# A graph layer's edge loop: destination products from a DRAM table, one silu for two layers, 72 and 72 columns

## The chip, the cores and the metric

The kernel runs on one core of one Trainium2 chip. The metric is the device time of one execution, in microseconds. The core's engines work at the same time, each from its own instruction queue: TensorE (PE) multiplies matrices into PSUM, VectorE (DVE) and ScalarE (ACT) work element by element, GpSimd (POOL) issues the indirect gathers, and SyncE (SP) issues most other DMAs. Each engine's queue is worked off in order.

## The reference

One message-passing layer over 12500 nodes with 64 features and 400000 edges with 16 features, edges sorted by destination:

```python
m_in = concatenate([x[src], x[dst], edge_attr], axis=-1)       # 64 + 64 + 16
h = silu(m_in @ W1 + b1)                                       # 64
messages = silu(h @ W2 + b2)                                   # 64
agg = segment_sum(messages, dst, num_segments=12500)
out = layernorm(x + silu(concatenate([x, agg], axis=-1) @ W3 + b3))
```

Everything is in float32. W1 has three blocks of rows: W1a for the source, W1b for the destination, W1c for the edge's features, so that `m_in @ W1` is a sum of three products.

## The kernel before

Edges are worked off in tiles of 128, eight tiles to an octet (1024 edges), 391 octets (NO; the last has five tiles). Two tiles share the 128 partitions of one product: 64 features of the one above 64 of the other. Function `windows` builds everything; `general`, a fallback for other data, is not entered in these runs.

Edges are sorted by destination, so that an octet's destinations lie in a window of S = 48 nodes from a base node. For the destination's share of the first layer, `window_load` (SP) brings the window's 48 columns of transposed x, twice side by side, into `xr`; `window_product` (PE, L397) multiplies them with W1b into 96 rows; and `window_copy` (DVE, L402) multiplies by a mask that leaves the left half of the columns for one tile of a pair and the right half for the other, and writes the result into the first 96 rows of a 128x128 tile `xw`. The other 32 rows of `xw` hold W1c twice. There are three such tiles. `compare_dst` (DVE, L424) makes the one-hot rows `oh` that pick each edge's destination from the window, and the edges' features are loaded below them, so that a single matmul over 128 rows (`first_layer`, L441) adds destination and feature shares. `load` brings the destinations `dr` and the features once for every three octets.

The source's share has three ways. From octet RAW = 12, x W1a lies as a table `pa` in DRAM, and `gather` (POOL, L373) fetches 128 rows of it by one indirect DMA for each tile; first_layer adds them through the identity (L454). Some pairs of tiles are not gathered: `rows` fetches theirs with 16 single-row DMAs an octet on SP (L324), and `columns` copies columns of the transposed x, which is resident in SBUF as `xs`, one edge at a time into a tile `cx`, with DVE (L297) and ACT (L299); a matmul with W1a (L451) then takes its place. A pair of tiles has 256 columns. `ACOLS` = (32, 28) and `VCOLS` = (32, 32) say how many columns ACT and DVE copy in the two parts of an octet, together RATE = 124. Where an octet stands in the list `pairs`, its first two gathers are left out. Each copy's address comes from a register; the registers are filled by loads from an index tile `cxi` (L290), `LOADS` = (16, 8): sixteen in the first load of a part, eight in the others. DVE makes the addresses from the indices once for each pair of tiles (`address`, L359). In the first twelve octets the rows of x itself are gathered and multiplied.

The rest of `first_layer` is a silu on ACT with bias b1 (L458) into `h`. `second_layer` multiplies by W2 (L467, L469) and has its own silu (L473) into `m`. `add_up` (PE, L482) sums the messages with one-hot tiles `eh` from `compare_nodes` (DVE, L430), and `add_window` (DVE, L487) adds the window into `agg`. Finished nodes are worked off between the octets by the node steps (L504 to L552): statistics with L530, L533 and L534, division with L547.

The order on PE, ACT, DVE and SP is the program's order, under `tc.manual_schedule`; POOL's gathers run three octets ahead (AHEAD) in five buffers `ga`. In octet o the loop issues, among others: window_load(o+3), window_product(o+1), add_window(o-4), compare_dst(o+1), DVE's first columns, first_layer(o) with ACT's first columns before its silu, window_copy(o+1), compare_nodes(o+1), DVE's second columns, add_up(o-2), second_layer(o-1) with ACT's second columns before its silu, the addresses for octet o+2, and SP's rows.

Of the kernel before, what the change touches and what calls it, by code (L numbers as in the profile page):

```python
# [9 lines left out]
F32 = mybir.dt.float32  # L10
# [18 lines left out]
RAW = 12  # L29
TABLES = 7  # L30
ACOLS = (32, 28)
VCOLS = (32, 32)
ROWS = 16
LOADS = (16, 8)
XBASE = (0, 64 << 18)
XADDR = 36864
# [7 lines left out]
@with_exitstack  # L44
def kernel(
    ctx: ExitStack,
    tc: tile.TileContext,
    x: bass.AP,
    xt: bass.AP,
    src_c: bass.AP,  # L50
    src_row: bass.AP,
    dst_c: bass.AP,
    dst_row: bass.AP,
    attr_t: bass.AP,
    dst_2: bass.AP,
    attr_2: bass.AP,
    base: bass.AP,
    w1: bass.AP,
    b1: bass.AP,
    w2: bass.AP,  # L60
    b2: bass.AP,
    w3: bass.AP,
    b3: bass.AP,
    out: bass.AP,
    edges: int,
):

    nc = tc.nc
    N, D = x.shape  # L80

    const = ctx.enter_context(tc.tile_pool(name="const", bufs=1))
    dram = ctx.enter_context(tc.tile_pool(name="dram", bufs=1, space=DRAM))
    pa = dram.tile([N, D], F32, name="pa")
    badi = const.tile([1, 1], I32, name="badi")
    ident = const.tile([P, P], F32, name="ident")
    make_identity(nc, ident)

    with ExitStack() as inner:
        windows(inner, tc, ident, badi, pa, x, xt, src_c, src_row, dst_c, dst_row, attr_t, dst_2, attr_2, base, w1, b1, w2, b2, w3, b3, out, edges)  # L90

    flag = nc.values_load(badi[0:1, 0:1], min_val=0, max_val=2 * P,
                          skip_runtime_bounds_check_because="a count of partitions")
    with tc.If(flag > 0):
        general(tc, ident, x, xt, src_c, dst_c, dst_row, attr_t, w1, b1, w2, b2, w3, b3, out, edges)


def windows(ctx, tc, ident, badi, pa, x, xt, src_c, src_row, dst_c, dst_row, attr_t, dst_2, attr_2, base, w1, b1, w2, b2, w3, b3, out, edges):
# [33 lines left out]
    b1s = const.tile([P, 1], F32, name="b1s")  # L132
# [3 lines left out]
    for s in range(2):  # L136
        h = slice(s * D, (s + 1) * D)
        nc.scalar.dma_start(w1d[h, h], w1[0:D, :])
        nc.scalar.dma_start(b1s[h, :], b1.rearrange("(k o) -> k o", o=1))
# [65 lines left out]
    nc.vector.memset(mask[:, :D], 0.0)  # L205
    nc.vector.memset(mask[:, D:], 1.0)
# [29 lines left out]
    for k in range(3):  # L236
        t = fast.tile([P, P], F32, name=f"xw{k}")
        nc.vector.memset(t, 0.0)
        for q in range(2):
            nc.sync.dma_start(t[E + q * A:E + (q + 1) * A, q * D:(q + 1) * D], w1[2 * D:2 * D + A, :])  # L240
        xw.append(t)
# [6 lines left out]
    with tc.tile_pool(name="gat", bufs=AHEAD + 2) as gat, tc.tile_pool(name="drp", bufs=2) as drp, \  # L248
# [4 lines left out]
            tc.tile_pool(name="ps2", bufs=2, space=PSUM) as ps2, \  # L253
# [17 lines left out]
        def columns(o, eng, part):  # L271
            if o < RAW:
                return
            lo = (o - RAW) * RATE
            if eng == ENG.Activation:
                lo, n = lo + sum(ACOLS[:part]), ACOLS[part]
            else:
                lo, n = lo + sum(ACOLS) + sum(VCOLS[:part]), VCOLS[part]
            hi, todo = lo + n, n
            while lo < hi:  # L280
                j, e0 = lo // (2 * P), lo % (2 * P)
                if j >= len(pairs):
                    return
                n = min(hi - lo, P - e0 % P, LOADS[lo > hi - todo])
                if pairs[j] not in cols:
                    cols[pairs[j]] = cx.tile([P, P], F32, name="cx")
                t = cols[pairs[j]].bitcast(U8)
                s = e0 // P
                h = slice(s * D, (s + 1) * D)
                _, regs = nc.values_load_multi_w_load_instructions(  # L290
                    indices[j][0:1, e0:e0 + n], engines=(eng,), min_val=XBASE[s] + XADDR,
                    max_val=XBASE[s] + XADDR + 4 * (N - 1), skip_runtime_bounds_check_because="src names a node")
                for e, r in zip(range(e0 % P, e0 % P + n), regs):
                    to, frm = t[h, 4 * e:4 * e + 4], xb[h, ds(r - (XBASE[s] + XADDR), 4)]
                    if eng == ENG.DVE:

                        nc.vector.tensor_reduce(to, frm[:, :, None], AX.X, OP.max)  # L297
                    else:
                        nc.scalar.copy(to, frm)  # L299
                lo += n  # L300
# [85 lines left out]

        def window_load(o):
            if o % 4 == 0:
                bases(ENG.SP, o)
            xr = win.tile([D, 2, S], F32, name="xr")  # L390
            frm = xt[:, ds(winreg.pop((ENG.SP, o)), S)]
            nc.sync.dma_start(xr, frm[:, None, :].to_broadcast([D, 2, S]))
            winrow[o] = xr

        def window_product(o):
            pw = mis.tile([P, P], F32, name="mm")
            nc.tensor.matmul(pw[:E, :], winrow[o].rearrange("k s w -> k (s w)"), w1bb.rearrange("k s m -> k (s m)"),  # L397
                             start=True, stop=True)
            winrow[o] = pw

        def window_copy(o):
            nc.vector.tensor_tensor(xw[o % 3][:E, :], winrow.pop(o)[:E, :], mask[:E, :], op=OP.mult)  # L402

        def load(c, o0=0, o1=CT // OT):
# [6 lines left out]
            for k in range(2):  # L411
                nc.sync.dma_start(dr[k * S:(k + 1) * S, e], dst_2[k:k + 1, d].to_broadcast([S, e.stop - e.start]))
            nc.sync.dma_start(oh[E:, e], attr_2[:, d])

        hots = {}
# [18 lines left out]
        def first_layer(o):  # L434
# [5 lines left out]
            p1 = ps1.tile([P, OT // 2, P], F32, name="p1")  # L440
            nc.tensor.matmul(p1[:, :k], xw[o % 3], oh, start=True, stop=False, skip_group_check=True)  # L441
            if o < RAW:
# [4 lines left out]
                xg = work.tile([P, OT // 2, P], F32, name="m")  # L447
# [8 lines left out]
            columns(o, ENG.Activation, 0)  # L456
            h = work.tile([P, OT // 2, P], F32, name="h")
            nc.scalar.activation(h[:, :k], p1[:, :k], AF.Silu, bias=b1s)  # L458
            made[o] = h, eh

        def second_layer(o):
# [3 lines left out]
            h, eh = made.pop(o)  # L465
            p2 = ps2.tile([P, OT, D], F32, name="p2")
# [4 lines left out]
            columns(o + 1, ENG.Activation, 1)  # L471
            m = work.tile([P, OT, D], F32, name="m")
            nc.scalar.activation(m[:, :n2], p2[:, :n2], AF.Silu)  # L473
            made[o] = m, eh

        def add_up(o):
            c, t0, n, first, last = octs[o]
            m, eh = made.pop(o)
# [114 lines left out]
        tables = list(range(0, N, 8 * P))  # L593
        cuts = [SCT] + [min(t + 46 * OT, TILES) for t in range(SCT, TILES, 46 * OT)]
# [3 lines left out]
        with tc.manual_schedule(engines={ENG.PE, ENG.Activation, ENG.DVE, ENG.SP}):  # L598
            compare_dst(0)
            compare_nodes(0)  # L600
            for o in range(NO + 1):
# [32 lines left out]
                if o + 1 < NO:  # L634
                    window_product(o + 1)
# [9 lines left out]
                if o == 0:  # L645
                    nc.vector.tensor_copy(b2r, b2p[:, None, :].to_broadcast([3, OT, D]))
                if o + 1 < NO:
                    window_copy(o + 1)
                    compare_nodes(o + 1)
# [10 lines left out]
                if o >= 1:  # L660
                    for c in tables[(o - 1) * per:o * per]:
                        table(c)
                if o >= 2:
                    add_up(o - 2)
                if o >= 1:
                    second_layer(o - 1)
# [298 lines left out]
```

## Time and profile before

| quantity | value |
|---|---|
| median of 10 runs | 3438.23 us (3437.63 to 3441.43) |
| the profiled execution | 3438.32 us, span 3436.1 us |
| granted TensorE clock, mean | 0.774 |
| PE busy | 2527.6 us, 74% |
| DVE busy | 2505.9 us, 73% |
| ACT busy | 2743.8 us, 80% |
| POOL busy | 2573.2 us, 75% |
| DMA | 229.98 MB, 67 GB/s in the mean |

The span runs from the first to the last instruction of the profiled execution. Busy time is time in which the engine itself works; what its queue does alone (register loads, semaphore waits, issuing DMAs) is not in it. In the group lines, a count is followed by the busy time in us and the mean duration in ns of one instruction; since instructions overlap, count times mean can exceed the busy time. After the second bar stands the engine's idle time just before such instructions and what ended most of it. "issue" is idle time that ended without any semaphore that the profile shows. In the waits, the three numbers are the total in us, how often, and the longest. In the timeline, the numbers are start and length in us, and a bracket gives the idle time before the piece.

### The profile page before, as it was taken

The numbers are of one execution on the slowest core, as the hardware profiler recorded it, in microseconds if no ns is written. First come the engines' busy times: TensorE is split into PE (matmuls) and PEld (weight loads), VectorE is DVE, ScalarE is ACT, GpSimd is POOL, SyncE is SP. The second block draws the span as 40 slices with busy tenths as digits, with TensorE's granted clock in tenths as the row PEclk, the third lists the DMA queues.
The fourth block names the chain that finished last, engine by engine and source line by source line (L and its number), as shares of the span: only waits on it lengthen the run. The fifth ranks groups of instructions, "written<-read, shape, count | busy, mean of one in ns | idle before, by whom it ended". The sixth has DMA issues, their size and how long they took to land. (4 is left out here: it accounts for less than half of the span.)

```text
span 3436.1 us, 107486 instructions
## 1 busy us (share of the span) xinstructions
PE 2527.6 (74%) x15131; PEld 1788.9 (52%) x15131; DVE 2505.9 (73%) x26395; ACT 2743.8 (80%) x23402; POOL 2573.2 (75%) x2724
## 2 busy tenths in 40 slices
PE   6877877767777777777677776767767777777676
PEld 4555555545555455555454554545545555555454
DVE  2487768777787777777777777777777777777775
ACT  2388878788888788887888878888888787887884
POOL 7777777777777777777777777777777777777774
PEclk8887777787877777777777778787788787777777
DMA  6533333223233322323323332332232333233232
GB/s 124 126 65 64 62 66 62 62 59 70 62 65 70 64 60 61 70 61 61 70 61 67 68 66 59 63 68 60 62 69 64 68 67 62 61 61 69 59 73 47
DMA packets 203943, 229.98 MB, mean 67 GB/s; under 512 B 133612, under 2 KB 141988, under 8 KB 202324
## 3 DMA queue, kind: packets, MB, share of 16 engines
q1 hardware_dynamic: 101528, 122.61, 16.0%
q0 software_dynamic: 86880, 89.14, 14.1%
q10 hardware_dynamic: 14812, 11.26, 1.4%
q14 instruction: 595, 4.87, 0.5%
q8 instruction: 128, 2.10, 0.3%
HBM read 216.36 MB, written 6.40 MB: 65 GB/s over the span
## 5 line engine op out<-in xcount | busy, mean ns | idle before, releaser
L373 POOL DMA_INDIRECT ga<-pa,sc x2619 | 2480.1, 947 | 798.6 <-issue 711.7
L299 ACT COPY cx<-xs 64x4 uint8 x22560 | 2236.2, 189 | 142.8 <-issue 112.0
L297 DVE TENSOR_REDUCE cx<-xs 64x4 uint8 x24032 | 1774.5, 150 | 552.0 <-issue 472.9
L441 PE MATMUL p<-oh,xw 128*128 128x512 f32 (+1 forms) x782 | 627.8, 896 | 315.9 <-DVE xw L402 313.1
L454 PEld LDWEIGHTS p<-ident,ga 128*128 128x128 f32 x2620 | 477.1, 252 | 368.5 <-issue 329.2
L454 PE MATMUL p<-ident,ga 128*128 128x128 f32 x2620 | 512.1, 341 | 192.9 <-DMA ga<-pa,sc 191.9
L469 PE MATMUL p<-w2d,h 128*128 128x128 f32 x3126 | 579.2, 342 | 0.0
L469 PEld LDWEIGHTS p<-w2d,h 128*128 128x128 f32 x3126 | 487.7, 238 | 110.5 <-issue 110.5
L482 PE MATMUL pg<-eh,m 128*64 128x48 f32 x6250 | 310.9, 250 | 308.3 <-DVE agg L487 258.2
L458 ACT ACTIVATE h<-p,b1s 128x512 f32<-128x512 f32 x391 | 268.8, 687 | 313.6 <-PE p L454 254.7
L482 PEld LDWEIGHTS pg<-eh,m 128*64 128x64 f32 x6250 | 265.2, 162 | 382.9 <-issue 168.8
L424 DVE TENSOR_TENSOR oh<-dr,wrow 96x512 f32<-96x512 int32 x391 | 264.0, 675 | 151.2 <-DMA dr<-in_dst 99.5
L441 PEld LDWEIGHTS p<-oh,xw 128*128 128x128 f32 x782 | 156.7, 250 | 411.8 <-DVE xw L402 381.2
L473 ACT ACTIVATE m<-p 128x512 f32<-128x512 f32 x391 | 232.2, 594 | 78.1 <-PE p L469 68.3
L397 PE MATMUL mm<-w1bb,xr 64*96 64x128 f32 x782 | 226.7, 380 | 67.4 <-DMA xr<-in_xt 52.2
L430 DVE TENSOR_TENSOR eh<-wrow,dc 128x384 f32<-128x384 f32 x391 | 211.1, 540 | 0.0
L397 PEld LDWEIGHTS mm<-w1bb,xr 64*96 64x96 f32 x782 | 120.3, 201 | 135.8 <-issue 49.6
L467 PE MATMUL p<-b2r,one 3*128 3x512 bf16 x391 | 173.0, 442 | 0.0
L451 PEld LDWEIGHTS p<-cx,w1d 128*128 128x128 f32 x364 | 94.3, 259 | 137.5 <-issue 137.5
L487 DVE TENSOR_TENSOR agg<-agg,pg 128x48 f32 x391 | 78.3, 200 | 108.0 <-PE mm L517 45.9
L402 DVE TENSOR_TENSOR xw<-mm,mask 96x128 f32<-96x128 f32 x391 | 108.9, 278 | 12.2 <-PE mm L397 6.3
L373 POOL DMA_INDIRECT ga<-in_x,sc x96 | 91.0, 948 | 30.7 <-issue 27.4
(81 smaller groups left out, 758.6 us busy)
## 6 DMA issues: line engine op xcount, KB each, us to landing
rx<-pa SPq DMA_DIRECT2D x5888, 0.2 KB
dr<-in_dst SPq DMA_DIRECT2D x260, 288.0 KB
ga<-pa,sc POOLq DMA_INDIRECT x2619
oh<-in_attr SPq DMA_DIRECT2D x130, 192.0 KB
xr<-in_xt SPq DMA_DIRECT2D x391, 24.0 KB
xs<-in_xt ACTq DMA_DIRECT2D x12, 512.0 KB
pa<-v ACTq DMA_DIRECT2D x12, 256.0 KB
xa<-in_x SPq DMA_DIRECT2D x24, 128.0 KB
```

The source lines that it names most:

```text
L297: nc.vector.tensor_reduce(to, frm[:, :, None], AX.X, OP.max)
L299: nc.scalar.copy(to, frm)
L373: nc.gpsimd.indirect_dma_start(out=ga[:, i, :], out_offset=None, in_=x if o < RAW else pa[:, :], in_offset=bass.IndirectOffsetOnAxis(ap=sc ...
L397: nc.tensor.matmul(pw[:E, :], winrow[o].rearrange("k s w -> k (s w)"), w1bb.rearrange("k s m -> k (s m)"), start=True, stop=True)
L424: nc.vector.tensor_tensor(oh[:E, :], dr[:, e:e + w], wn[:E, o:o + 1].to_broadcast([E, w]), op=OP.is_equal)
L430: nc.vector.tensor_tensor(eh[:, :n], row[:, None, :].to_broadcast([P, n, S]), rel[:, t0:t0 + n, None].to_broadcast([P, n, S]), op=OP.is_equal)
L441: nc.tensor.matmul(p1[:, :k], xw[o % 3], oh, start=True, stop=False, skip_group_check=True)
L454: nc.tensor.matmul(p1[:, i, :], g2.rearrange("p s d -> p (s d)"), ident, start=False, stop=(i == k - 1), skip_group_check=True)
L458: nc.scalar.activation(h[:, :k], p1[:, :k], AF.Silu, bias=b1s)
L469: nc.tensor.matmul(p2[:, 2 * i:2 * i + 2, :].rearrange("p s d -> p (s d)"), h[:, i, :], w2d, start=False, stop=(i == k - 1), skip_group_ch ...
L473: nc.scalar.activation(m[:, :n2], p2[:, :n2], AF.Silu)
L482: nc.tensor.matmul(pg[s * D:(s + 1) * D, :], m[:, i, :], eh[:, i, :], start=(i < 2), stop=(i >= n - 2), skip_group_check=True)
```

## The change

Three things change together.

- The destination's share. A second table in DRAM, `pw1b`, gets a row for each node: 64 zeros, then x W1b + b1. `table_b` computes 256 nodes of it in one octet, from octet 8 on, 50 times, with PE, an ACT copy and a DMA from ACT's queue. From octet OWN = 60 on, `window_load` reads an octet's 96 rows of 512 bytes straight into `xw`: the first 48 from the start of a row, the other 48 from 64 numbers further, so that the zeros of the next row follow the values. Window product, mask and copy are left out there. Up to octet 59 the window product remains, with one more matmul for b1, and the silu has no bias any more. The halves of the mask and of the destinations are exchanged. There are five `xw` tiles.
- One silu for two layers. PSUM tiles of 2 x 512 numbers hold the first layer of octet o and the second layer of octet o-1; `silus` applies one ACT operation to both. Second layer o-1 moves before it in the octet's order, and `add_up` after it. Where an octet is not full, there are two operations.
- Columns. ACOLS = (40, 32) and VCOLS = (40, 32): 72 columns on each of ACT and DVE instead of 60 and 64, RATE 144. The loads of addresses are of eight throughout. ACT's two parts both stand before the one silu.

```diff
+OWN = 60
+XWB = 5
 TABLES = 7
-ACOLS = (32, 28)
-VCOLS = (32, 32)
+ACOLS = (40, 32)
+VCOLS = (40, 32)
 ROWS = 16
-LOADS = (16, 8)
+LOADS = 8
 XBASE = (0, 64 << 18)
-XADDR = 36864
+XADDR = 37344
...
-    b1s = const.tile([P, 1], F32, name="b1s")
+    b1r = const.tile([1, 2, D], F32, name="b1r")
+    nc.scalar.dma_start(b1r, b1.rearrange("(o s k) -> o s k", o=1, s=1).to_broadcast([1, 2, D]))
...
-    nc.vector.memset(mask[:, :D], 0.0)
-    nc.vector.memset(mask[:, D:], 1.0)
+    nc.vector.memset(mask[:, :D], 1.0)
+    nc.vector.memset(mask[:, D:], 0.0)
...
+    pbs = []
+    for k in range(2):
+        t = fast.tile([P, 2, 2 * D], F32, name=f"pbs{k}")
+        nc.vector.memset(t, 0.0)
+        pbs.append(t)
+    for k in range(XWB):
         t = fast.tile([P, P], F32, name=f"xw{k}")
         nc.vector.memset(t, 0.0)
         for q in range(2):
-            nc.sync.dma_start(t[E + q * A:E + (q + 1) * A, q * D:(q + 1) * D], w1[2 * D:2 * D + A, :])
+            (nc.sync if k < 3 else nc.scalar).dma_start(t[E + q * A:E + (q + 1) * A, q * D:(q + 1) * D], w1[2 * D:2 * D + A, :])
...
-                n = min(hi - lo, P - e0 % P, LOADS[lo > hi - todo])
+                n = min(hi - lo, P - e0 % P, LOADS)
+                yield j, e0, n
+                lo += n
...
+        def table_b(c):
+
+            n = min(2 * P, NP - c)
+            k = (n + P - 1) // P
+            ps = mis.tile([P, 2, D], F32, name="mm")
+            t = pbs[c // (2 * P) % 2]
+            for i in range(k):
+                p = min(P, n - i * P)
+                nc.tensor.matmul(ps[:p, i, :], xs[0:D, c + i * P:c + i * P + p], w1ab[:, 1, :], start=True, stop=False)
+                nc.tensor.matmul(ps[:p, i, :], ones[:, :p], b1r[:, 0, :], start=False, stop=True)
+            if n == 2 * P:
+                nc.scalar.copy(t[:, :, D:], ps)
+                nc.scalar.dma_start(pw1b[c:c + n, :].rearrange("(i p) d -> p i d", p=P), t)
+                return
...
+            if o >= OWN:
+                v = pw1b[ds(winreg.pop((ENG.SP, o)), S), :]
+                v = bass.AP(tensor=v.tensor, offset=v.offset, ap=[[D, 2]] + list(v.ap))
+                nc.sync.dma_start(xw[o % XWB][:E, :], v)
...
-                             start=True, stop=True)
+                             start=True, stop=False)
+            nc.tensor.matmul(pw[:E, :], ones[:, :E], b1r.rearrange("o s k -> o (s k)"), start=False, stop=True)
...
-                nc.sync.dma_start(dr[k * S:(k + 1) * S, e], dst_2[k:k + 1, d].to_broadcast([S, e.stop - e.start]))
+                nc.sync.dma_start(dr[k * S:(k + 1) * S, e], dst_2[1 - k:2 - k, d].to_broadcast([S, e.stop - e.start]))
...
-            p1 = ps1.tile([P, OT // 2, P], F32, name="p1")
-            nc.tensor.matmul(p1[:, :k], xw[o % 3], oh, start=True, stop=False, skip_group_check=True)
+            both[o] = ps1.tile([P, 2, OT // 2, P], F32, name="p12")
+            outs[o] = work.tile([P, 2, OT // 2, P], F32, name="hm")
+            p1 = both[o][:, 0]
+            nc.tensor.matmul(p1[:, :k], xw[o % XWB], oh, start=True, stop=False, skip_group_check=True)
...
-            columns(o, ENG.Activation, 0)
-            h = work.tile([P, OT // 2, P], F32, name="h")
-            nc.scalar.activation(h[:, :k], p1[:, :k], AF.Silu, bias=b1s)
-            made[o] = h, eh
+            nodes_of[o] = eh
...
-            p2 = ps2.tile([P, OT, D], F32, name="p2")
+            h = made.pop(o)
+            if o + 1 == NO:
+                both[NO] = ps1.tile([P, 2, OT // 2, P], F32, name="p12")
+                outs[NO] = work.tile([P, 2, OT // 2, P], F32, name="hm")
+            p2 = both[o + 1][:, 1].rearrange("p i (s d) -> p (i s) d", s=2)
...
-            columns(o + 1, ENG.Activation, 1)
-            m = work.tile([P, OT, D], F32, name="m")
-            nc.scalar.activation(m[:, :n2], p2[:, :n2], AF.Silu)
-            made[o] = m, eh
+
+        def silus(o):
+
+            pp = both.pop(o)
+            hm = outs.pop(o)
+            columns(o, ENG.Activation, 0)
+            columns(o, ENG.Activation, 1)
+            k = [-(-octs[q][2] // 2) if 0 <= q < NO else 0 for q in (o, o - 1)]
+            if k == [OT // 2, OT // 2]:
+                nc.scalar.activation(hm, pp, AF.Silu)
+            else:
+                for j in range(2):
+                    if k[j]:
+                        nc.scalar.activation(hm[:, j, :k[j]], pp[:, j, :k[j]], AF.Silu)
+            made[o] = hm[:, 0]
+            messages[o - 1] = hm[:, 1].rearrange("p i (s d) -> p (i s) d", s=2)
 
         def add_up(o):
             c, t0, n, first, last = octs[o]
-            m, eh = made.pop(o)
+            m, eh = messages.pop(o), nodes_of.pop(o)
...
+        tables_b = list(range(0, NP, 2 * P))
+        assert 8 + len(tables_b) + 2 <= OWN
...
                     first_layer(o)
                 if o == 0:
                     nc.vector.tensor_copy(b2r, b2p[:, None, :].to_broadcast([3, OT, D]))
+                if o + 1 < min(OWN, NO):
+                    window_copy(o + 1)
                 if o + 1 < NO:
-                    window_copy(o + 1)
                     compare_nodes(o + 1)
                 columns(o, ENG.DVE, 1)
                 if o == 1:
@@ -660,10 +719,13 @@
                 if o >= 1:
                     for c in tables[(o - 1) * per:o * per]:
                         table(c)
+                if o >= 1:
+                    second_layer(o - 1)
+                silus(o)
+                if 8 <= o < 8 + len(tables_b):
+                    table_b(tables_b[o - 8])
                 if o >= 2:
                     add_up(o - 2)
-                if o >= 1:
-                    second_layer(o - 1)
                 address(o + 2)
                 raddress(o + 2)
                 rows(o)
```

## The prediction

> **What bounds the kernel now.** I read the page's first part and the waits, then the groups, then the trace record by record, because no engine is busy over 80%.
>
> ```profile
> PE 2527.6 (74%) x15131; PEld 1788.9 (52%) x15131; DVE 2505.9 (73%) x26395; ACT 2743.8 (80%) x23402; POOL 2573.2 (75%) x2724
> POOL ga L373 <- issue: 739.2, 2424, 0.3
> DVE cx L297 <- issue: 472.9, 1447, 0.9
> PEld p L441 <- DVE xw L402: 381.2, 258, 3.2
> ACT cx L299 <- issue: 112.0, 272, 0.8
> POOL ga L373 <- PE p L454: 11.6, 38, 0.3
> ```
>
> POOL's waits are its own: a pause of 0.3 us after each gather, and only 11.6 us for PE. A gather starts every 1.25 us from 3.0 us to 3401 us (947 ns busy, 0.30 pause), and 2715 x 1.25 is 3394 of the span's 3436. POOL sets the pace. After the twelfth octet it makes 2619 gathers in 379 octets, 6.91 each, so 8.64 us an octet; the first column loads of consecutive octets on DVE lie 8.63 apart on average.
>
> DVE is the next to look at, for its "issue" waits.
>
> ```profile
> L373 POOL DMA_INDIRECT ga<-pa,sc x2619 | 2480.1, 947 | 798.6 <-issue 711.7
> L299 ACT COPY cx<-xs 64x4 uint8 x22560 | 2236.2, 189 | 142.8 <-issue 112.0
> L297 DVE TENSOR_REDUCE cx<-xs 64x4 uint8 x24032 | 1774.5, 150 | 552.0 <-issue 472.9
> L402 DVE TENSOR_TENSOR xw<-mm,mask 96x128 f32<-96x128 f32 x391 | 108.9, 278 | 12.2 <-PE mm L397 6.3
> ```
>
> The 24032 columns keep DVE busy only 74 ns each, but each needs an address in a register, and those come by loads that its queue executes itself:
>
> ```profile
> L290 DVEq TENSOR_LOAD <-cxi x2391: 339/597/1350, 149.2 to 3389.2; - x200
> L290 ACTq TENSOR_LOAD <-cxi x2352: 304/546/1270, 150.6 to 3389.3; - x196
> ```
>
> What such a load does to the queue shows in DVE's timeline, in an octet whose second part happens to be cut into eights:
>
> ```profile
> 2022.91 0.27 DVE L402 TENSOR_TENSOR xw<-mm,mask 96x128 f32<-96x128 f32 x1
> 2023.10 0.54 DVE L430 TENSOR_TENSOR eh<-wrow,dc 128x384 f32<-128x384 f32 x1
> 2023.57 0.58 DVE L297 TENSOR_REDUCE cx<-xs 64x4 uint8 x8
> 2024.31 0.62 DVE L297 TENSOR_REDUCE cx<-xs 64x4 uint8 x8 [0.17 <-issue]
> 2025.25 0.62 DVE L297 TENSOR_REDUCE cx<-xs 64x4 uint8 x8 [0.31 <-issue]
> 2026.17 0.62 DVE L297 TENSOR_REDUCE cx<-xs 64x4 uint8 x8 [0.30 <-issue]
> ```
>
> Groups of eight start 0.92 to 0.94 apart, though their work takes 0.62: a load takes 0.597, then the eight copies are sent off in 0.32, and the next load begins only then. Over the whole trace, the 866 loads of eight that are followed by another in the same part lie 0.918 apart in the median and never under 0.913; the 682 loads of sixteen lie 1.665 apart. So a column costs DVE's queue 115 ns in eights and 104 in sixteens, whatever the 74 ns of work.
>
> **DVE's octet, now and after.** Now: two parts of 16+8+8 columns are 2 x (1.665 + 2 x 0.918) = 7.0; extra loads where a pair's half ends, and the instructions between the parts, bring it to 7.7 without any wait. It has 0.9 us to spare under POOL's 8.64.
>
> After: 40 and 32 columns, loaded by eights only, are nine groups, 9 x 0.918 = 8.26. Between the parts, L402 and L430 now add 0.075 to the queue; from octet 60 only the latter is left: 0.04. At the octet's end (address arithmetic, base registers, the sum into `agg`, the destination compare), the shortest tenths of the intervals beyond the last group are 0.25 plain, 0.42 with the addresses of a new pair, 0.68 with the base registers. Pairs grow from 182 to 211 (RATE 124 to 144), so 0.56 of 376 octets start one, and a quarter load bases: 0.25 + 0.56 x 0.17 + 0.25 x 0.43 = 0.45. The node steps of 24 groups add 2.0 us where the statistics stand and 0.2 at each division, 53 us in all: 0.14 an octet. Sum 8.26 + 0.04 + 0.45 + 0.14 = 8.89 us. Bounds: 8.75 if the node steps vanish in the queue's other waits; 9.1 if the waits for `dr` stay (99.5 + 39.1 us idle before L424, that is 0.37 an octet, about half of it kept). I take 8.89, because nearly every term is a measured interval without a wait.
>
> [...]
>
> **POOL.** The 29 further pairs take two gathers each away: 2561 after the twelfth octet, 58 x 1.25 = 72 us less, 8.45 us an octet. This gain is real only if nothing else needs more than 8.45. DVE does, so POOL gets idle time, waiting for a `ga` buffer, and none of the 72 us is seen.
>
> **ACT.** Twelve more columns an octet; eights cost its queue 0.80 (median of 836, copies 96 ns apart), nine of them 7.24. The two silus (688 and 594 ns) become one of 1024 elements: 256 elements take 385 ns and 512 take 594, so 594 + 2 x 209 = 1.01 us; at most the old sum 1.28. Copies of 72 x 0.096 plus that are 7.9 to 8.2 us, hidden under DVE's 8.89. If DVE's cover were gone, ACT would still fit under POOL's 8.45. The one silu waits for first layer o and second layer o-1; both depend on the silu before, some 7 us earlier, and PE needs about 2.3 us for the second layer's matmuls. Behind that wait stand the next octet's address loads and columns, and PE's `add_up` waits for it; 4 buffers of sums and 5 of `eh` separate it from DVE.
>
> The table is ACT's exception. In octets 8 to 57 ACT copies 128x128 numbers (265 ns, by L184's row of that size) after PE's eight short passes, waits for the copy, issues a DMA (0.38, as `pa<-v` takes), and only then loads addresses. From the silu's start: 1.2 for the passes at 0.14 each (L181's busy time; the silu's 1.01 lies beside them), 0.27, 0.4. So 1.9 us of its queue are lost, 7.24 + 1.9 + 0.1 = 9.24 against DVE's 8.89, and in the 46 octets that also have columns 46 x 0.35 = 16 us. From both sides: 0, if ACT's head start (its columns begin 4 us before DVE's in the median) absorbs it, to 40, if PE comes late.
>
> **PE and SP.** Window products (0.58 us an octet) and the xw wait of 381 us go after octet 59. What is late next for PE is `oh` and the gather; PE has 26% idle, so nothing is gained. The added bias passes for the first 60 octets hide there too. SP loses the 0.62 us `xr` issue and gets one of 96 rows of 512 bytes; between the 0.37 of the attributes' 32 rows and 0.62, so no loss. Its 16 row DMAs at 0.324, an address load of 1.42 and the rest make some 8.0 to 8.4 us. It is close behind, but under 8.89. The 24 KB more per octet are 8 MB on 230 at a DMA share of 0.31; the load is issued three octets ahead. If it were late, PE would pay at most what `xr` costs it now, 95 us. The first such read waits once for the table's last write, at most one octet of SP's lead.
>
> **Sum.** The profiled execution took 3438.3 (span 3436.1), the median of the runs shown is 3438.2. Up to the first column load 149 us, paced by POOL's gathers of raw octets and so the same (within 5: four more memsets and DMA issues). 376 x 8.89 = 3343. Table 16. From the last column load to the end 47 now, partly POOL's last full octets, which will be ahead by then: 40. Together 3548, plus 2 around the span: 3550 us, 3.3% slower.
>
> **Rivals.**
> *POOL stays the bound, faster.* One mechanism: DVE's queue takes eights in less than 0.87 us, or runs ahead during its 0.68 and 0.54 us compares. It decides when DVE's octet falls under 8.45. Time 3438 - 72 = 3366. For it: DVE is 73% busy. Against: not one of 866 intervals under 0.913, and 9 of them alone are 8.22, which leaves 0.23 for all else, while the shortest octet end is 0.234.
> *No change.* DVE at 8.63 an octet, 0.26 under my sum: the octet's end and the node steps would have to be half of what was measured. 3431 to 3445.
> *ACT becomes the bound throughout.* Its single silu would have to expose the way from silu to second layer and back: 2.3 us on top of 7.24, over 9.5 with the silu's start: 149 + 376 x 9.5 + 40 = 3761. For it: ACT waits 254.7 us for PE in L458 now. Against: those columns stand between the two silus.
>
> **How the numbers follow.** The forecast with 8.75 to 9.1 and the table at 0 to 40 us gives 149 + 3290 + 40 + 2 = 3481 to 149 + 3422 + 40 + 40 + 2 = 3653; trimmed at the top, where both extremes meet, 3475 to 3625: 0.80. Slower by less, 3445 to 3475: 0.03. ACT throughout or the top, above 3625: 0.06. No change: 0.03. POOL's pace: 0.08. A measurement of this kernel tells about 0.2%, 7 us, from no change. Faster 0.08, same 0.03, slower 0.89; the range 3475 to 3625 holds 0.80.
>
> **What would show it.** Right: the gathers' mean distance grows past 1.30 us with POOL waits on PE's `p`; DVE's groups of eight stand 0.92 apart throughout; DVE's octets lie 8.8 to 9.1 apart; ACT idles before the silu, except before octet 58, where its octets are over 9 us. Wrong: gathers still every 1.25 us to the end (then the loads are hidden after all), or DVE idle for PE or DMA rather than "issue" while ACT's queue is unbroken.

## The result and the profile after

The changed kernel takes 3777.22 us (median of 8 runs, 3770.86 to 3789.47), the kernel before 3438.26 us in the same session (28 runs): a ratio of 1.0988, 95% interval 1.0978 to 1.0997. The forecast was 3550 us. The sign is right, and the loss is three times as large as forecast, outside the range. The profiled execution took 3792.95 us (span 3791.2), 16 us above the median; all sums below are made against this span.

The page of the changed kernel, first part and costliest groups. In a group line the three numbers after the first bar are busy time in us and mean ns of one, then comes the idle time before such instructions and what ended it:

```profile
PE 2659.3 (70%) x14985; PEld 1897.9 (50%) x14985; DVE 2701.5 (71%) x29094; ACT 3133.6 (83%) x27519; POOL 2514.2 (66%) x2666
...
L390 POOL DMA_INDIRECT ga<-pa,sc x2561 | 2421.3, 945 | 1185.9 <-issue 678.6
L317 ACT COPY cx<-xs 64x4 uint8 x27016 | 2703.3, 188 | 172.3 <-issue 105.7
L315 DVE TENSOR_REDUCE cx<-xs 64x4 uint8 x27000 | 2053.9, 148 | 822.7 <-issue 776.2
...
L524 ACT ACTIVATE hm<-p 128x1024 f32<-128x1024 f32 x389 | 396.6, 1020 | 169.2 <-PE p L513 165.2
```

The gathers are 58 fewer, as worked out, but 1186 us of idle time now stand before them instead of 799. From 700 to 3500 us they start 1.374 us apart in the mean, before 1.2515.

The waits (us in total, times, longest us) name what came last:

```profile
PE pg L538 <- DVE agg L543: 898.7, 300, 6.4
DVE cx L315 <- issue: 776.2, 2421, 0.9
...
POOL ga L390 <- PE p L498: 440.9, 166, 13.6
```

POOL waits for PE (440.9 us, before 11.6). PE waits for DVE's `agg`, which frees the PSUM tile `pg`. DVE, from 700 to 3740 us, waits for its own queue and for hardly anything else; the two longest of its waits there are:

```profile
DVE cx L315 <- issue: 673.7, 2107, 0.8
DVE agg L543 <- DVE cx L315: 7.2, 29, 0.6
```

The chain of waits therefore ends at DVE's queue, as forecast. The same queue has 3375 address loads instead of 2391, all of eight:

```profile
L298 ACTq TENSOR_LOAD <-cxi x3377: 542/547/1005, 180.9 to 3743.2; - x199
L298 DVEq TENSOR_LOAD <-cxi x3375: 591/596/1089, 180.8 to 3752.2; - x199
```

The first and last start in the second of these lines cut the span into stages. The end of octet 57 comes from the loads record by record:

| stage | before, us | forecast, us | after, us |
|---|---|---|---|
| up to the first column load on DVE | 149.2 | 149 | 180.8 |
| octets 12 to 57, with the table | 392.0 (8.52 each) | 425 (9.24 each) | 509.3 (11.07 each) |
| octet 58 to the last column load | 2848.1 | 2934 (8.89 each) | 3062.1 |
| the rest | 46.8 | 40 | 38.9 |

The octets from 60 to 380 lie 9.30 us apart on DVE (before 8.66). So the forecast missed 32 us in the start, 84 in the table's octets and 128 afterwards.

DVE's timeline in one plain octet shows both what was expected and what was missed:

```profile
2010.55 0.20 DVE L543 TENSOR_TENSOR agg<-agg,pg 128x48 f32 x1
2010.67 0.68 DVE L466 TENSOR_TENSOR oh<-dr,wrow 96x512 f32<-96x512 int32 x1
2011.27 0.58 DVE L315 TENSOR_REDUCE cx<-xs 64x4 uint8 x8
2012.17 0.59 DVE L315 TENSOR_REDUCE cx<-xs 64x4 uint8 x8 [0.32 <-issue]
2013.10 0.28 DVE L315 TENSOR_REDUCE cx<-xs 64x4 uint8 x3 [0.33 <-issue]
2013.54 0.40 DVE L315 TENSOR_REDUCE cx<-xs 64x4 uint8 x5 [0.17 <-issue]
2014.36 0.59 DVE L315 TENSOR_REDUCE cx<-xs 64x4 uint8 x8 [0.42 <-issue]
2015.28 0.59 DVE L315 TENSOR_REDUCE cx<-xs 64x4 uint8 x8 [0.33 <-issue]
```

Groups stand 0.92 apart, but one of them is split (three copies, a pause, five copies), and the next group starts 1.26 after it. Of the 2240 intervals between loads of eight in octets 60 to 380 (the octets counted wherever a mean is given below), 7.8% are longer than 1.1 us, most of them 1.25 to 1.3. The median is 0.921, the mean 0.955. The kernel before has the same pauses in 8.4% of its intervals: median 0.918, mean 0.951. They were in the trace that the forecast was made from.

The pauses have a pattern. Number the records of DVE in the trace, register loads and semaphore instructions included, from 0 in order of their start. Copies of one group start 0.06 to 0.07 us apart; every one that starts over 0.15 us after the one before it (166 in the changed kernel, 134 in the kernel before) comes at a number that leaves 63 when divided by 128, and such a number lies in 159 of the 174 long intervals of the changed kernel, but in only 17 of the 2066 short ones. So most of the long intervals are a cost of every 128th instruction in DVE's queue. Why the queue pauses there, no run shows. DVE has some 87 records an octet, which makes 0.68 such pauses and, at 0.35 us each, an estimated 0.24 us an octet.

In the table's octets, ACT's timeline shows the second thing:

```profile
410.66 1.02 ACT L524 ACTIVATE hm<-p 128x1024 f32<-128x1024 f32 x1
411.58 0.26 ACT L415 COPY pbs<-mm 128x128 f32<-128x128 f32 x1
411.87 0.38 ACTq L416 DMA_DIRECT2D pw1b<-pbs  x1
412.90 4.05 ACT L317 COPY cx<-xs 64x4 uint8 x40 [1.06 <-issue]
...
430.06 1.02 ACT L524 ACTIVATE hm<-p 128x1024 f32<-128x1024 f32 x1
430.98 0.26 ACT L415 COPY pbs<-mm 128x128 f32<-128x128 f32 x1
434.75 0.38 ACTq L416 DMA_DIRECT2D pw1b<-pbs  x1
435.78 7.33 ACT L317 COPY cx<-xs 64x4 uint8 x72 [4.54 <-issue]
```

In the first octet the table's DMA goes out 0.29 us after its copy starts. In the second it goes out 3.77 us after, with a semaphore instruction ahead of it in the queue, and everything on ACT waits behind it: 4.54 us idle before the next copy. Of octets 12 to 56, each with such a DMA, 26 issue it 1.2 to 1.5 us after the silu's start and take 9.78 us to the next silu; the other 19 issue it 2.1 to 7.2 us after, and take 13.1.

### The profile page after: what moved, and what is told of

Same layout as the page of the kernel before. It is cut to its first block, busy times and chain, and to the rows that moved or that the text cites. A ratio compares the mean times of both kernels' runs of the same rounds, so it can differ in the third digit from the quotient of the medians.

```text
span 3791.2 us, 115732 instructions
## 1 busy us (share of the span) xinstructions
PE 2659.3 (70%) x14985; PEld 1897.9 (50%) x14985; DVE 2701.5 (71%) x29094; ACT 3133.6 (83%) x27519; POOL 2514.2 (66%) x2666
## 5 line engine op out<-in xcount | busy, mean ns | idle before, releaser
L317 ACT COPY cx<-xs 64x4 uint8 x27016 | 2703.3, 188 | 172.3 <-issue 105.7
L315 DVE TENSOR_REDUCE cx<-xs 64x4 uint8 x27000 | 2053.9, 148 | 822.7 <-issue 776.2
L538 PE MATMUL pg<-eh,hm 128*64 128x48 f32 x6250 | 364.9, 279 | 902.2 <-DVE agg L543 898.7
L538 PEld LDWEIGHTS pg<-eh,hm 128*64 128x64 f32 x6250 | 306.8, 189 | 972.0 <-DVE agg L543 958.9
L485 PE MATMUL p<-oh,xw 128*128 128x512 f32 (+1 forms) x782 | 730.4, 1033 | 0.6 <-PE pg L538 0.5
L513 PE MATMUL p<-w2d,hm 128*128 128x128 f32 x3126 | 519.5, 315 | 141.5 <-ACT hm L524 141.3
L513 PEld LDWEIGHTS p<-w2d,hm 128*128 128x128 f32 x3126 | 440.9, 218 | 272.9 <-ACT hm L524 164.6
L524 ACT ACTIVATE hm<-p 128x1024 f32<-128x1024 f32 x389 | 396.6, 1020 | 169.2 <-PE p L513 165.2
L495 PE MATMUL p<-cx,w1d 128*128 128x128 f32 x422 | 125.2, 397 | 0.0
L376 DVE TENSOR_SCALAR cxi<-cxi 1x128 int32<-1x128 int32 x422 | 81.8, 243 | 1.6
```

The source lines that it names most:

```text
L485: nc.tensor.matmul(p1[:, :k], xw[o % XWB], oh, start=True, stop=False, skip_group_check=True)
L495: nc.tensor.matmul(p1[:, 0, :], w1d, cols.pop(o), start=False, stop=False, skip_group_check=True)
L513: nc.tensor.matmul(p2[:, 2 * i:2 * i + 2, :].rearrange("p s d -> p (s d)"), h[:, i, :], w2d, start=False, stop=(i == k - 1), skip_group_ch ...
L524: nc.scalar.activation(hm, pp, AF.Silu)
L538: nc.tensor.matmul(pg[s * D:(s + 1) * D, :], m[:, i, :], eh[:, i, :], start=(i < 2), stop=(i >= n - 2), skip_group_check=True)
```

## The experiments

The expectations name theories by letters. A: DVE's queue, with a load for every eight columns, paces the octets from 58 on, and the table's steps on ACT those before. B: ACT's chain around the one silu does, and the columns alone are cheap. C, in the runs on the table: the table, or its DMA on ACT's queue, is not what costs there. D: SP's queue of row loads is next in line, and shows as soon as DVE's is relieved. Unless said otherwise, a diff is against the changed kernel. The kernel before took 3438.3, 3433.6, 3432.3 and 3433.2 us in the four sessions; ratios are to the one of the same session.

### Columns alone, on the kernel before

```diff
-ACOLS = (32, 28)
-VCOLS = (32, 32)
+ACOLS = (40, 32)
+VCOLS = (40, 32)
...
-LOADS = (16, 8)
+LOADS = (8, 8)
```

> The kernel before with the columns alone: ACOLS = VCOLS = (40, 32), loads of eight. No table, two silus, ACT's columns in two parts as before. Theory A (DVE's queue): 9.3 us an octet as in the changed kernel, 149 + 376 x 9.3 + 42 = 3690 us. Theory B (one silu): ACT and PE are as before, so POOL's pace, 3366 to 3440 us.

3727.54 us, ratio 1.0864 (1.0846 to 1.0882): 87% of the loss from the columns and their loads of eight, without table or one silu. The octets lie 9.435 us apart. B is out. It came 38 us above A's 3690; A had counted this queue too low here as well. The waits of this run:

```profile
DVE cx L297 <- issue: 709.4, 2243, 0.7
...
PE p L441 <- DVE xw L402: 490.6, 305, 3.1
POOL ga L373 <- PE p L454: 391.7, 192, 10.5
```

It is the same chain as in the changed kernel, POOL for PE, PE for DVE, DVE for its queue; with the window copy still on DVE, PE waits for `xw`.

### The number of columns, or the loads of eight

On the kernel before, the two differences one at a time:

```diff
-ACOLS = (32, 28)
-VCOLS = (32, 32)
+ACOLS = (40, 32)
+VCOLS = (40, 32)
...
-LOADS = (16, 8)
+LOADS = (16, 16)
```

> The kernel before with 72 and 72 columns as in the run of the columns alone (3727 us, 9.43 us an octet), but with loads of sixteen. Theory A (the loads of eight on DVE's queue): four groups of sixteen and one of eight, 7.58 + 0.07 + 0.6 and pauses of 0.3, 8.55 to 8.7 us an octet, which is POOL's 8.45 no more but close: 3400 to 3470. If the columns' number and not the load's size matters: 9.3 to 9.4, about 3710.

```diff
-LOADS = (16, 8)
+LOADS = (8, 8)
```

> The kernel before with its own 60 and 64 columns, loaded by eights only. A (DVE's queue pays for each load of eight): eight groups an octet, six intervals of 0.951 us, one of 1.02 between the parts and an octet's end of 1.62 are 8.35 us, under the 8.66 of before, so 3430 to 3475. If eights cost something that does not depend on the number of columns (the two further loads an octet on ACT, or the register loads as such), the octets go over 9 us and the time over 3550.

72 and 72 in sixteens: 3463.82 us, ratio 1.0103 (1.0078 to 1.0128), octets 8.74. Eights on the old columns: 3433.18 us, ratio 1.0002 (0.9993 to 1.0012), octets 8.655: DVE's 8.35 is not seen under POOL's 8.64. With the run above this is a square:

| ratio to before | 60 and 64 columns | 72 and 72 columns |
|---|---|---|
| sixteens (left: before's own mixture) | 1 | 1.0103 |
| eights | 1.0002 | 1.0864 |

Neither part costs much alone; both together lift DVE's queue from under POOL's pace to 0.8 us above the 8.64. A's times for both runs held; its octet for the first, 8.55 to 8.7 us, was just exceeded.

### Sixteens in the changed kernel

```diff
-LOADS = 8
+LOADS = 16
```

> The changed kernel with one number changed: LOADS = 16, so that an octet's 72 columns on each of DVE and ACT come by 16+16+8 and 16+16 instead of nine loads of eight. Theory A (DVE's queue sets the pace after octet 58: 9.28 us an octet, of which nine groups of eight are 8.26): four groups of sixteen at 1.665 and one of eight at 0.918 are 7.58, 0.68 less, so about 8.6 us an octet, near POOL's 8.45, and 330 x 0.65 = 215 us less, about 3560 us; the table's octets 12 to 57 stay at 11 us. Theory B (ACT's single silu and the way over PE and back set the pace): no change, 3750 to 3790 us.

3702.4 us, ratio 1.0799 (1.0762 to 1.0835): between A and B. DVE's median octet fell to 8.62, but the mean only to 9.065, since a quarter of the octets take over 9.7. The waits now include DMAs that SP issues for three octets at once (`PE p` for `oh<-in_attr` 72.8 us, `DVE oh` for `dr<-in_dst` 64.7 between 700 and 3500 us). A alone does not explain this; from here D was tested.

### The old columns in the changed kernel

```diff
-ACOLS = (40, 32)
-VCOLS = (40, 32)
+ACOLS = (32, 28)
+VCOLS = (32, 32)
...
-LOADS = 8
+LOADS = (16, 8)
...
-            hi = lo + n
+            hi, todo = lo + n, n
...
-                n = min(hi - lo, P - e0 % P, LOADS)
+                n = min(hi - lo, P - e0 % P, LOADS[lo > hi - todo])
```

> The changed kernel with the columns of the kernel before: ACOLS (32, 28), VCOLS (32, 32), loads (16, 8); table, one silu and five xw tiles as in the changed kernel. Theory A: after octet 58 POOL's pace of before, 8.64 us an octet; the start 30 us longer as in the changed kernel, and octets 12 to 57 slower than 8.64 by the table's lost time on ACT, 46 x 0.5 to 1.8: 3490 to 3560 us. Theory B: well over 9 us an octet after octet 58, above 3600 us.

3612.16 us, ratio 1.0516 (1.0485 to 1.0546), 9.0 us an octet: above A's range, though DVE has its old 124-column rate back. Its median octet is 8.14, and a quarter of them take over 10.3. The waits say for what:

```profile
DVE cx L315 <- issue: 532.2, 1566, 0.9
...
PE p L485 <- DMA oh<-in_attr: 218.2, 77, 5.4
...
DVE oh L466 <- DMA dr<-in_dst: 170.1, 65, 4.8
```

Both are SP's loads. They are issued late: the compare that needs them starts 5.2 us (median) after the issue of the first, in the changed kernel 10.1. SP's own queue is unbroken. Set against the kernel before, between 700 and 3300 us, an octet's address load takes 1.50 us of it (before 1.31), the read of `xw` 0.68 (the `xr` that it replaces 0.63), and the semaphore waits ahead of row DMAs 0.30 (before 0.19). The number of 9.0 lies in B's range, but ACT is not what is waited for.

### Fewer rows for SP

```diff
-ROWS = 16
+ROWS = 8
...
-LOADS = 8
+LOADS = 16
```

> The changed kernel with loads of sixteen, as before (9.07 us an octet after octet 58, 3702 us), and with ROWS = 8: SP fetches 8 single rows an octet instead of 16, so that POOL has 24 gathers more. Theory D (with sixteens SP's queue is the pace: 16 rows at 0.324, an address load of 1.5, the xw read of 0.68 and the waits of row DMAs behind the three large loads make 9.05): SP falls to about 6 us, and the octet to the larger of DVE's 8.4 to 8.7 and POOL's 8.53: 8.6 to 8.7, 130 us less, about 3570. If SP is not it: POOL's 24 gathers change nothing either, 9.0 to 9.1 us an octet, 3700.

3514.62 us, ratio 1.0241 (1.0221 to 1.0260), octets 8.607, although POOL has more gathers. Against the run in sixteens with 16 rows this is 0.46 us an octet. D is confirmed: the octet is as it expected, and the time falls by 188 us instead of 130. SP's queue has room again: between 700 and 3300 us its semaphore instructions take 0.79 us an octet, in the run with 16 rows 0.05. What is left over the kernel before lies in front: octets 12 to 57 take 10.4 us, and the first column load comes at 165 us.

### The table

Without the table every octet makes its window product itself:

```diff
-OWN = 60
+OWN = 10 ** 6
...
-                if 8 <= o < 8 + len(tables_b):
-                    table_b(tables_b[o - 8])
```

> The changed kernel without the table: OWN beyond the last octet and table_b never called, so that every octet has a window product with its bias matmul and a window copy, as octets 0 to 59 of the changed kernel; silu, columns and loads as in the changed kernel. Theory A (the table's DMAs on ACT's queue, which wait for DMAs of other queues, cost octets 12 to 57 some 1.8 us each, and the table's part of the start some 10): 83 + 10 less there, 0.04 us more on DVE's queue in 330 octets, about 3695 us, octets 12 to 57 at the 9.3 of the rest. Theory C (these octets are slow because PE is: bias matmuls and a lower granted clock): they stay at 10 us or more, about 3750 us or above.

3729.07 us, ratio 1.0861 (1.0843 to 1.0879), against 1.0988 with the table. The start falls to 150.7 us and octets 12 to 57 to 9.5, as A said; but the other octets rise to 9.40, since the window copy is back on DVE (the step between the parts 1.026 us instead of 0.988, and more long intervals: 12.9% over 1.1 us instead of 7.8%, mean 0.964 instead of 0.955). So the table costs some 44 us net (0.0127 of the time), although it wins 0.1 us in each octet that it serves. A's 3695 had counted 0.04 us of this 0.1. The ratio agrees with that of the columns alone, 1.0864: one silu for two layers, with its order and buffers, costs nothing here.

Next, the table's DMA from POOL's queue instead of ACT's, nothing else:

```diff
-                nc.scalar.dma_start(pw1b[c:c + n, :].rearrange("(i p) d -> p i d", p=P), t)
+                nc.gpsimd.dma_start(pw1b[c:c + n, :].rearrange("(i p) d -> p i d", p=P), t)
...
-                nc.scalar.dma_start(pw1b[c + i * P:c + i * P + p, :], t[:p, i, :])
+                nc.gpsimd.dma_start(pw1b[c + i * P:c + i * P + p, :], t[:p, i, :])
```

> The changed kernel, but the table's 50 writes are issued from POOL's queue instead of ACT's; all else the same. In the changed kernel's octets 12 to 57 the ACT queue stands up to 6 us before such a DMA, on a semaphore that it shares with DMAs of SP's queue. Theory A (that wait makes the octets 11.1 us): without it ACT needs 7.24 + 1.3 + 0.55 or so, under DVE's 9.4, so these octets fall to 9.4 to 9.8 and the time by 46 x 1.4 = 65 us, to about 3710. Theory C (PE, with bias and table matmuls at a lower clock, or ACT's copy itself, is the cause): octets stay at 10.8 to 11.1 us, 3760 to 3785 us.

3730.69 us, ratio 1.0874 (1.0855 to 1.0894). Octets 12 to 57 fall from 11.07 to 9.95 us, 51 us together, the start to 158 us; the octets from 60 on stay at 9.30. ACT's wait for nothing but its own queue, in the changed kernel and in this one:

```profile
ACT cx L317 <- issue: 105.7, 180, 6.9
```

```profile
ACT cx L317 <- issue: 40.3, 164, 0.6
```

The waits of up to 6.9 us are gone. A's 3710 was not reached, but C, as the whole cause, is out. Why these octets still take 0.65 us more than the later ones is not settled; ACT now waits for PE there, for instance 13.0 us before the table's copies between 200 and 700 us.

### One silu, two silus, and the table, in sixteens with 8 rows

The kernel before and the changed kernel without its table, both with 72 and 72 columns in sixteens and 8 rows; between them stand only the one silu with its order, the separate b1 matmul and the two further `xw` tiles. The first, against the kernel before:

```diff
-ACOLS = (32, 28)
-VCOLS = (32, 32)
+ACOLS = (40, 32)
+VCOLS = (40, 32)
-ROWS = 16
-LOADS = (16, 8)
+ROWS = 8
+LOADS = (16, 16)
```

> The kernel before with 72 and 72 columns in sixteens and 8 rows an octet by SP. With 16 rows this took 3464 us at 8.74 us an octet. A (DVE's queue paces it, 2.5 intervals of 1.725 us and the rest): nothing is gained from SP, 8.6 to 8.74 us, 3415 to 3470. D (SP paced it): POOL's 8.53 us, under 3410.

The second, against the changed kernel, with the table left out as above:

```diff
-OWN = 60
+OWN = 10 ** 6
...
-ROWS = 16
-LOADS = 8
+ROWS = 8
+LOADS = 16
```

> The changed kernel without its table (every octet makes its product itself), in sixteens and with 8 rows an octet by SP; only the one silu of two layers and the two further buffers remain of the change, beside the 72 and 72 columns. Against the same with the table (3515 us, of which octets 12 to 57 took 10.3 us instead of 8.6 and the start 165 us): 46 x 1.7 + 15 = 93 us less, about 3425 to 3450. If the table's octets are not what costs there, over 3490. Against the two silus with the same columns and rows: within 20 us if one silu for two costs nothing; over 30 us more if it exposes the second layer.

Two silus: 3451.47 us, ratio 1.0060 (1.0045 to 1.0075), octets 8.70. One: 3450.48 us, ratio 1.0052 (1.0037 to 1.0068), octets 8.66. They are the same. The one silu is neither a gain nor a loss; ACT waits for PE before it only 60.5 us in the whole run:

```profile
L524 ACT ACTIVATE hm<-p 128x1024 f32<-128x1024 f32 x389 | 396.0, 1018 | 65.0 <-PE p L513 60.5
```

Against the same with the table (ratio 1.0241) the table costs 0.0189, some 65 us. In the profiled executions it is 70: 10 in the start, 73 in octets 12 to 57 (10.4 us each against 8.8), less 13 later. In the kernel before, the 8 rows won little (1.0103 to 1.0060), so SP was at most a small part of the limit of 72 and 72 columns there. DVE's queue is the rest: in the run with 8 rows DVE waits, between 700 and 3300 us, 457.0 us for its own queue and some 31 us for all else.

### 72 and 64 columns on the kernel before

```diff
-ACOLS = (32, 28)
+ACOLS = (40, 32)
...
-LOADS = (16, 8)
+LOADS = (16, 16)
```

> The kernel before with 72 columns on ACT, 64 on DVE (RATE 136, 23 fewer gathers or so than before) and loads of sixteen. DVE's queue 7.7 us, ACT 8.3, SP 8.4 to 8.6, POOL 1.2515 x (8 - 152/128) = 8.53. Theory A and D: the octet is 8.55 to 8.6, 3400 to 3425, a little faster than before. If ACT's two silus with waits hold it: 8.8 or more, slower than before.

The same, with `ROWS = 8` as well:

> The kernel before with 72 columns on ACT, 64 on DVE, all in sixteens, and 8 instead of 16 rows an octet by SP. With 16 rows this took 3435 us at 8.71 us an octet. D (SP's queue held it): SP loses eight row loads of 0.32 us, POOL needs 1.2515 x (8 - 144/128) = 8.60 us an octet and becomes the bound again: 8.60 to 8.65, 3385 to 3425. If ACT's or DVE's queue held it, the octets stay at 8.7 and the time at 3430 to 3450.

With 16 rows: 3435.06 us, ratio 1.0004 (0.9993 to 1.0014), octets 8.71; neither expectation exactly. With 8 rows: 3427.03 us, ratio 0.9982 (0.9973 to 0.9991), octets 8.585. The waits of the first, then of the second:

```profile
DVE oh L424 <- DMA dr<-in_dst: 192.3, 89, 4.5
```

```profile
PE p L454 <- DMA ga<-pa,sc: 461.6, 302, 6.3
...
DVE oh L424 <- DMA dr<-in_dst: 9.6, 10, 2.0
```

With 16 rows SP's loads came late; with 8 they do not, PE waits for the gathers, and POOL sets the pace again (1.250 us a gather). The time is still above D's 3425: POOL's gathers run on to 3384 us, while DVE's last column is loaded at 3350, and the end takes 75 us. This is the fastest kernel of the study, 0.18% under the kernel before, which is below the 0.2% that the forecast called measurable.

## Why the prediction was right or wrong

**What bounds the kernel now, and what takes over: right.** POOL set the pace, and DVE's queue took it over through its address loads. The square of columns and loads shows it by taking each away. POOL's 72 us were indeed not seen.

**A load and its copies in line: right.** The copies behind a load take their addresses from the registers that it fills, and in the changed kernel the first of them starts 0.09 us (median) after the load's end. Whether an instruction behind a load that needs none of its registers would have to wait too, no run here tests. What was queued ahead of a load does go on during it: DVE is at work in 1462 of the 2018 us that its 3375 address loads take in the changed kernel. What the forecast put into its sum holds: a load (0.597 us) and the sending of its eight copies (0.32) stand in line, groups with 0.62 us of work stand 0.92 apart, and eights instead of sixteens cost some 260 us on 72 and 72 columns, the copies being the same.

**DVE's octet, 8.89 us: the step "nine groups, 9 x 0.918 = 8.26" failed.** It multiplied a median where nothing on the path can absorb the longer intervals; there the mean is what adds up. Measured are seven intervals of 0.955, one between the parts of 0.988 and an octet's end of 1.624, its group included: 6.685 + 0.988 + 1.624 = 9.30. Against the forecast's terms the groups and the step between the parts hold 0.29 more (7.673 against 8 x 0.918 + 0.04 = 7.384), and the octet's end 0.12 more (1.624 against 0.918 + 0.45 + 0.14 = 1.508). With the mean of the kernel before, 0.951, in place of its median, the same sum gives 9 x 0.951 + 0.04 + 0.59 = 9.19 us; 330 octets of that are 3033 us, against 3062 measured and 2934 forecast. Most of this term was to be read before: it is the long intervals, most of them at every 128th instruction, that the median leaves out. The bound of 9.1 was too low for the same reason.

**The table, "16 us, 0 to 40": wrong.** Octets 12 to 57 took 84 us more than forecast. One part is ACT's own octet, which takes 9.78 us instead of 9.24 when the DMA goes out at once, 25 us over 46 octets: 1.69 until the first address load (forecast 1.9 and 0.1), 6.65 for the eight intervals between loads (0.83 each in the mean; the forecast took the median, 0.80), and 1.44 from the last load to the next silu, where the forecast counted one more interval of 0.80 although the silu stands behind the group's copies. The other part was not in the sum: 19 of these octets issue the table's DMA late, by some 64 us together. The records say for what. In the changed kernel's trace the DMAs of ACT's and SP's queues are counted on the same eight semaphores (100 and 102 to 108), and the waiting instruction on ACT waits for the semaphore that its own DMA then counts on. In the octet shown, where it is 108, SP issued row loads on that semaphore at 430.14 and 432.98 us; its last update before ACT's DMA came at 434.67, and the DMA went at 434.75. So it is in all 19: the last DMA before on that semaphore is a row load of SP's, and ACT's DMA goes 0.08 us after the semaphore's last update. That this wait costs time where it stands, on ACT's queue, the run with POOL's queue showed (51 us of those octets). POOL's gathers are counted on other semaphores (111 to 118 in the changed kernel); if its table writes are too, that run took away the sharing as well. The DMA was priced at its 0.38 us of issue, and what its counter might wait for was left out.

**The start, "149 us, within 5": wrong by 32.** It was argued from POOL's gathers, but PE is the busy one there: 148.8 of the first 181 us, before 113.7 of 149, at a granted clock of 0.73 instead of 0.82. In every one of the 14 profiles the start is PE's busy time and 31 to 35 us more. The seven profiles with the program of the kernel before, which does the same work up to there, show what the clock does: 149, 149 and 142 us at 0.82, 0.82 and 0.83, 135 at 0.89, and 127 to 130 in the three at 0.95. The added passes show beside these: with the table's DMA on POOL's queue the start takes 158 us at 0.82, 9 more than the kernel before at that clock, and in the run without table in sixteens 155 at 0.88, 20 more than the 135 at 0.89. An estimate from these: 9 to 20 of the 32 us are added work, and the rest goes with the lower clock. Why the clock was lower, no run shows; the forecast let the added passes hide and did not look at the clock.

**SP, "8.0 to 8.4 us … so no loss": wrong, and without effect on this result.** SP's queue needs about 9.0 us in the changed kernel (9.07 in sixteens, 9.00 with the old columns, against 8.61 when eight rows are taken away), under DVE's 9.30. In the form before it needs 8.7, POOL's own pace. So SP's queue and POOL stood within 0.1 us of each other in the kernel before. This also means that POOL's 8.45 was not to be had by relieving DVE alone: by these numbers SP's queue, with 16 rows, would have kept the rival "POOL stays the bound" from its 3366 us.

**ACT's single silu, "1.01 us", hidden: right.** It measures 1020 ns, and one silu or two made no difference in two pairs of runs. The rival with ACT as the bound throughout gave 3761 us, 16 us from the result, but by another mechanism: ACT's loads run 10.7 us (median) ahead of DVE's, and its whole wait for PE before the silu is 165 us. A rival that meets the time is not thereby right.

**The signs that were to show it.** Gathers over 1.30 us apart with POOL waiting for PE's `p`: yes, 1.374 and 440.9 us. Groups 0.92 apart throughout: in the median, not in the mean. Octets of 8.8 to 9.1: no, 9.30. Octets over 9 us before 58: yes, 11.07. ACT idle before the silu: little, 169 us in all.

## What to carry to other kernels

A stage that is paced by a queue costs the mean of its intervals, pauses included; the median belongs only where slack absorbs the rest, and the difference of 0.035 us between the two was worth 0.3 us an octet here. Before a step is put on another queue, price not only its issue (0.38 us here) but what its DMA's counter can be waiting for (up to 6 us here), and which engine's work stands behind it. And where three resources are within a few per cent of one another, moving load off one (20 more columns an octet in place of gathers) needs room on all the others: the same 72 and 72 columns cost the kernel before 1% in sixteens and 9% in eights.

## What the runs showed of the hardware that was not expected

- Between copies on DVE that wait for nothing, about 8% of the groups of eight hold a pause of some 0.35 us, in both kernels. Nine in ten of these long intervals contain a 128th instruction of DVE's queue; in the changed kernel without its table (13% long) it is about half, and what the other half is stays open.
- A DMA of 128 KB on ACT's queue, whose issue takes 0.38 us, went out up to 6 us late in 19 of 45 octets, each time 0.08 us after the last update of a semaphore that a row load of SP's had just used.
- The granted TensorE clock did not set the whole time: 3448.8 us of span at 0.749 and 3445.2 at 0.823 for two kernels with the same columns, and 3715.1 at 0.683 beside 3719.8 at 0.764 for two others. It shows in the start, where PE is busy most of the time: 127.5 us at 0.95 and 149.2 at 0.82 for the same work.
